# A selective-scan kernel of four layers: later pair sums, 64-row loads, all of them on one queue, new step positions and more buffers

## The chip, the cores and the metric

The kernel runs on one NeuronCore of a Trainium2 chip. The metric is the device time of one execution in microseconds (us). All times of instructions come from one profiled execution of the kernel; the kernel's own time is the median of three executions that were not profiled.

A core has five engines that take their instructions in order, each from its own queue: PE (matrix products; its weight loads are listed as PEld), DVE (vector), ACT (scalar functions), POOL (GpSimd) and SP, which computes nothing and issues DMAs. "SPq" and "ACTq" in a profile mean the queue of that engine: what it waits for or issues.

## The reference

The input has four images of 64 x 64 positions and 192 channels, in float32. Four residual layers follow each other, each on a group-normalised or layer-normalised input. Layers 0, 1 and 3 are selective state-space layers; layer 2 is a Toeplitz mixing layer that the change doesn't touch. What matters here is the scan that layers 0, 1 and 3 share, with 384 inner channels (192 in layer 3) and 16 states for each channel:

```python
def step(h, inp):
    d_t, b_t, c_t, u_t = inp
    dA = jnp.exp(d_t[:, :, None] * A)
    h = dA * h + (d_t * u_t)[:, :, None] * b_t[:, None, :]
    y = jnp.einsum('nds,ns->nd', h, c_t)
    return (h, y)
```

Here d_t is a softplus of a projection (called delta), and b_t and c_t are projections of the convolved input u. In layers 0 and 3 one scan runs over all 4096 positions of an image, in four directions (rows, columns, and both reversed). In layer 1 a sequence is one line of 64 positions, forward and reversed, of rows and then of columns; its output is y + u * D, times silu(z), times an output matrix, and the reversed directions are added to what the forward ones left in DRAM:

```python
u = silu(conv1d(u) + cb)
y = y + u * D
y = y * silu(z)
return einsum('nld,cd->nlc', y, out_w)
```

## The kernel before

**Units and jobs.** A job is a chunk of 512 positions in one direction. Layer 1 has 128 jobs (4 directions x 4 images x 8 chunks) that run as one list: 32 forward jobs on rows, 32 reverse jobs on rows, 32 forward and 32 reverse jobs on columns. Layers 0 and 3 have 32 jobs for each image. A job is cut into units (t, p, c): t is a block of 128 channels, c one half of it (64 channels), and p one of four groups of states; on the 128 partitions lie 64 channels x 2 halves of the states, and a unit's tile of 1024 columns holds two states for each. So a job of layers 0 and 1 has 24 units, one of layer 3 has 12.

**What one unit does.** `feed` builds the input b = delta * u * B in PSUM by matrix products with the diagonal matrices `diag` (L374, PE), and dA by two exponentials (L397, ACT). For the units named in `direct` (p = 3, in layer 1 and 3 for both c, in layer 0 for c = 1 only) b comes from POOL instead (`spread`, L347: dtu times B, both spread over the partitions by DMA), and dA is put into PSUM. `scan` runs the recurrence on DVE (L407 in layer 1, one instruction; L414 in layers 0 and 3, two, with a carry that ACT copies at L424 for the next job) and multiplies by C on POOL (L418). `collect` sums over states on PE with the matrix `fold` (L443), two units (a pair) in each of two steps n = 0, 1.

**Order of the work.** `run_jobs` writes the units down one after the other. At position i it feeds unit i + 2, scans unit i, spreads unit i + 3, and takes one entry from `waiting` to collect; a pair enters `waiting` when its second unit has been scanned, so its two sums stand at positions i + 1 and i + 2. Then the steps due at i are written; a step that returns a function gets that function run at i + 1. A job's other work stands at fixed positions before or after its first unit: `load` of its input, `input_of` (convolution, layer 1), `project` to B, C and delta, `turn_b`, `step_size` and `finish` (softplus, L269; then dtu = delta * u at L275, on POOL in layer 1, on DVE in layers 0 and 3), `turn` (transpose of dtu, L235 and L289), `gate` (z, L839), `gated` (u * D + y, L852, then times z, L853) and `out` (L877 to L888). In a layer 1 reverse job `earlier` (L869) loads what the forward direction left, and `out` adds to it. A scheduler then sets each engine's order from what was written and from its own times, so an instruction can stand a little earlier or later than written. Every DMA also waits for an earlier DMA that used the same one of eight completion semaphores.

**Loads.** `plan` gives each load a position: at least when its data is ready, at most 12 units ahead (`LEAD`), and, where its buffer has an earlier user, `behind` units after that user (3 in layers 0 and 3, 2 in layer 1). `fetch` issues them, all on SP: C (`c`, L335) and B (`bc`, L335), delta (`both`) and dtu (`dtu2`, called dtu in the profile where it is loaded). In layers 0 and 3 `both` and `dtu2` are copied from SBUF in pieces of at most 64 rows (L317). In layer 1 they come from DRAM, both halves of the partitions in one transfer of 128 rows of 2 KB:

```python
src = job["deltas" if name == "both" else "dtus"][key * 64 : (key + 1) * 64, :]
nc.sync.dma_start(one, src.unsqueeze(0).broadcast_to([2, 64, T]))
```

The stores that these loads read are issued by ACT for B, C (L226) and delta (L272), and by SP for dtu (L295). Layer 1 has buffers c=4, bc=2, diag=4, both=4, dtu2=2 and seven h tiles; layers 0 and 3 have three h tiles (and five hc tiles).

Of the kernel before, what the change touches and what calls it, by code (L numbers as in the profile page):

```python
# [7 lines left out]
F32 = mybir.dt.float32  # L8
# [8 lines left out]
N = 16  # L17
R = 12
E = R + 2 * N
T = 512  # L20
# [5 lines left out]
EARLY = 3  # L26
# [10 lines left out]
class Kernel:  # L37
# [66 lines left out]
    def run_jobs(self, jobs, pools):  # L104


        G = jobs[0]["DI"] // 64
        order = []
        for t in range(-(-G // 2)):
            order += [(t, *one) for one in (TWO if 2 * t + 1 < G else ONE)]  # L110
        units = [(k, *one) for k in range(len(jobs)) for one in order]
        per = len(order)
        steps = {}
        for k, job in enumerate(jobs):
            for at, step in self.prepare(job, pools) + job["steps"]:
                steps.setdefault(k * per + at, []).append(step)
        for at, load in self.plan(jobs, order, pools):
            steps.setdefault(at, []).append(load)
        start, end = min(steps), max(len(units) + 3, max(steps) + 1)
        waiting, rest = [], []  # L120
        for i in range(min(start, -EARLY), end + 4):
            if 0 <= i + AHEAD < len(units):
                k, t, p, c = units[i + AHEAD]
                self.feed(jobs[k], t, p, c, pools)
            todo = waiting[:1]
            if 0 <= i < len(units):
                k, t, p, c = units[i]
                after = self.scan(jobs[k], t, p, c, pools)
                if after is not None:
                    steps.setdefault(i + 1, []).insert(0, after)  # L130
            if 0 <= i + EARLY < len(units):
                k, t, p, c = units[i + EARLY]
                if c in jobs[k]["direct"].get(p, ()):
                    self.spread(jobs[k], t, p, c, pools)
            if 0 <= i < len(units):
                if (i + 1) % 2 == 0:
                    waiting += [(units[i][0], [one[1:] for one in units[i - 1 : i + 1]], n) for n in range(2)]


            if todo:  # L140
                k, two, n = waiting.pop(0)
                self.collect(jobs[k], two, n, pools)
                if n and two[1][1] == LAST:
                    steps.setdefault(i, []).append(lambda job=jobs[k], t=two[0][0]: job["add"](t))
            now, rest = rest + steps.pop(i, []), []
            for step in now:
                after = step()
                if after is not None:
                    rest.append(after)
        assert not rest and not steps and not waiting  # L150

    def plan(self, jobs, order, pools):


        uses, ready = {}, {}
        for k, job in enumerate(jobs):
            job["cbc"], job["bbc"], job["diag"], job["both"], job["dtu2"] = {}, {}, {}, {}, {}
            job["dtuT"] = {}
            when = {name: k * len(order) + at for name, at in job["when"].items() if isinstance(at, int)}

            near = 2 if job["carry"] is not None else 5
            dtu = when["finish"] + 3 if job["carry"] is not None else when["store"] + 5
            for j, (t, p, c) in enumerate(order):
                i, g = k * len(order) + j, 2 * t + c
                direct = c in job["direct"].get(p, ())
                reads = [("c", p, i, when["project"] + 6), ("both", g, i - AHEAD, when["finish"] + near)]
                if direct:
                    reads += [("bc", p, i - EARLY, when["project"] + 6), ("dtu2", g, i - EARLY, dtu)]
                else:
                    reads.append(("diag", p, i - AHEAD, when["turn_b"] + 5))  # L170
                for name, key, at, after in reads:
                    first, _ = uses.setdefault(name, {}).get((k, key), (at, at))
                    uses[name][k, key] = first, at
                    ready[name, k] = after
        loads = []
        for name, of in uses.items():
            bufs, turn = pools["bufs"][name], sorted(of, key=of.get)
            for j, (k, key) in enumerate(turn):
                first = of[k, key][0]
                at = max(ready[name, k], first - LEAD)  # L180
                if j >= bufs:
                    at = max(at, of[turn[j - bufs]][1] + pools["behind"])
                one = lambda part=None, job=jobs[k], name=name, key=key: self.fetch(job, name, key, pools, part)
                if name == "diag":


                    at = max(ready[name, k], first - (LEAD_DIAG if k else NB))
                    if j >= bufs:
                        at = max(at, of[turn[j - bufs]][1] + 3)
                    loads += [(first, at + part, lambda part=part, one=one: one(part)) for part in range(NB)]  # L190
                    at += NB - 1
                else:
                    loads.append((first, at, one))
                assert at < first, (name, k, key, at, first)
        return [one[1:] for one in sorted(loads, key=lambda one: one[0])]

    def prepare(self, job, pools):

        nc = self.nc
# [14 lines left out]
        def projected(ps):  # L214
# [8 lines left out]
            else:  # L223
                by_half = job["bc"].rearrange("a (h l) -> h a l", h=2)
            for h in range(2):
                nc.scalar.dma_start(by_half[h], xd[h * 64 : h * 64 + 2 * N, :])  # L226
            job["delta"] = prep.tile([P, NT, T], F32, name="delta", bufs=1)
            job["dtu"] = prep.tile([P, NT, T], F32, name="dtu", bufs=1)
            if P < 128:
# [37 lines left out]
        def finish():  # L267
            delta = job["delta"]
            nc.scalar.activation(delta, delta, AF.Softplus)  # L269
            if job["carry"] is None:  # L270
                job["deltas"] = self.bcd.tile([DI, T], F32, name="delta_dram")
                nc.scalar.dma_start(job["deltas"].rearrange("(t p) l -> p t l", p=P), delta)  # L272

            def after():
                (nc.gpsimd if job["carry"] is None else nc.vector).tensor_mul(job["dtu"], delta, job["u"])  # L275

            return after

        def turn(t):
            ps = mm.tile([128, NB, P], F32, name="dtu_ps", tag="mm")  # L280
# [16 lines left out]
        when = job["when"]  # L297
# [7 lines left out]
    def fetch(self, job, name, key, pools, part):  # L305
# [13 lines left out]
        elif name in ("both", "dtu2"):  # L319
            one = job[name][key] = pools[name].tile([128, T], F32, name=name)  # L320
            src = job["deltas" if name == "both" else "dtus"][key * 64 : (key + 1) * 64, :]
            nc.sync.dma_start(one, src.unsqueeze(0).broadcast_to([2, 64, T]))
        elif name == "diag":
            if part == 0:
                job["diag"][key] = pools["diag"].tile([128, NB, 4, 128], F32, name="diag")
# [74 lines left out]
    def scan(self, job, t, p, c, pools):  # L400
# [1 line left out]
        rev, carry, g = job["rev"], job["carry"], 2 * t + c  # L402
        way = slice(None, None, -1) if rev else slice(None)
        b, dA, direct = job["fed"].pop((t, p, c))
        h = pools["work"].tile([128, 2 * T], F32, name="h", bufs=7 if carry is None else 3)
        if carry is None:
            nc.vector.tensor_tensor_scan(h[:, way], dA[:, way], b[:, way], 0.0, ALU.mult, ALU.add)  # L407
        else:
# [143 lines left out]
    def ss2d_scan(self, pre, u_d, y_d, P, NT, ways, A, dtb):  # L552
# [3 lines left out]
        with (  # L556
# [10 lines left out]
            tc.tile_pool(name="s_y", bufs=2, space=PSUM) as yp,  # L567
        ):
            pools = {"prep": prep, "work": work, "c": cp, "diag": dp, "both": both, "mm": mm, "b": bp, "y": yp,
                     "bc": bcp, "dtu2": dtu2, "bufs": bufs, "behind": 3}  # L570
            jobs = []
            carry = {
                (g, p): pw.tile([128, 2], F32, name=f"carry{g}_{p}", bufs=1)
                for g in range(DI // 64) for p in range(PAIRS)
            }
            when = {
                3: dict(load=-33, project=-29, turn_b=-27, step_size=(-21, -19, -17), finish=-15,
                        turn=(-13, -11, -9), direct={3: (1,)}),
                2: dict(load=-25, project=-21, turn_b=-19, step_size=(-17, -16), finish=-14,
                        turn=(-9, -8), direct={3: (0, 1)}),  # L580
            }[NT]
# [122 lines left out]
    def mamba(self, x_in):  # L704
# [6 lines left out]
        done = [[self.dram.tile([C, L], F32, name=f"m_out{i}_{b}") for b in range(B)] for i in range(2)]  # L711

        both_w = [self.dram.tile([P, NT, C], F32, name=f"m_both_w{i}") for i in range(4)]
        bufs = dict(c=4, bc=2, diag=4, both=4, dtu2=2)
        with (
            tc.tile_pool(name="n", bufs=2) as pn,
            tc.tile_pool(name="n_ps", bufs=2, space=PSUM) as psum,
# [27 lines left out]
        with (  # L745
# [12 lines left out]
            tc.tile_pool(name="m_y", bufs=2, space=PSUM) as yp,  # L758
        ):
            pools = {"prep": prep, "work": work, "c": cp, "diag": dp, "both": both, "mm": mm, "b": bp, "y": yp,  # L760
                     "bc": bcp, "dtu2": dtu2, "bufs": bufs, "behind": 2}
            fixed = [once.tile([P, 2 * T], F32, name=f"dA{j}") for j in range(3)]
            zero = once.tile([P, 2 * ROWS], F32, name="zero")
            nc.gpsimd.memset(zero, 0.0)
# [13 lines left out]
    def mamba_job(self, pw, pin, mm, i, begin, rev, w, x, done, both_w, c, fixed, zero):  # L778
# [69 lines left out]
        def gated(t):  # L848

            def after():  # L850
                u, z = job["u"][:, t, :], job["z"][:, t, :]
                nc.vector.scalar_tensor_tensor(u, u, w["D"][:, t : t + 1], job["y"][t], ALU.mult, ALU.add)  # L852
                nc.gpsimd.tensor_mul(z, z, u)  # L853

            return after

        def parts(m):

# [30 lines left out]

            return after  # L890

        when = dict(project=-24, turn_b=-22, step_size=(-20, -19, -17), finish=-15, turn=(-9, -2, 3), store=-11)
        each = lambda f, ats: [(at, lambda t=t: f(t)) for t, at in enumerate(ats)]
        steps = [(-50, weights)] if begin else []
        steps += [(-46, load)] + each(input_of, (-37, -34, -31)) + each(gate, (-4, -1, 1)) + each(out, (30, 33))
        if rev:
            steps += each(earlier, (25, 28))
        job.update(
# [327 lines left out]
```

## Time and profile before

| What | Value |
|---|---|
| Median of three executions | 31300.29 us (31296.12 to 31304.8) |
| The profiled execution | 31284.29 us, of which the span from first to last instruction is 31282.5 us |
| Layer 0, first to last job start | 168 us to 10244 us |
| Layer 1, first to last job start | 10763 us to 21834 us |
| Layer 3, first to last job start | 25136 us to 31034 us |
| Busy over the span: PE, DVE, ACT, POOL | 87%, 71%, 74%, 73% |
| Mean granted TensorE clock | 0.952 |

A job's start is taken from the copy `xd` on ACT (L216), of which there is one for each job. A line of the groups names source line, engine, operation and operands (out<-in), its count, busy time and mean duration, and then the idle time of the engine just before and what ended it. A line of the waits reads: who waited, for whom, us in total, how many times, the longest. A line of a window gives the length of the stretch, and busy time with the number of instructions in brackets for PE, PEld, DVE, ACT and POOL, then the granted clock, the share of time in which the DMA engines moved data, and GB/s. A line of the timeline has start, duration, engine, line, operation, and the idle time before it. Durations on PE end at modelled times, and matrix products overlap.

### The profile page before, as it was taken

The numbers are of one execution on the slowest core, as the hardware profiler recorded it, in microseconds if no ns is written. First come the engines' busy times: TensorE is split into PE (matmuls) and PEld (weight loads), VectorE is DVE, ScalarE is ACT, GpSimd is POOL, SyncE is SP. The second block draws the span as 40 slices with busy tenths as digits, with TensorE's granted clock in tenths as the row PEclk, the third lists the DMA queues.
The fourth block names the chain that finished last, engine by engine and source line by source line (L and its number), as shares of the span: only waits on it lengthen the run. The fifth ranks groups of instructions, "written<-read, shape, count | busy, mean of one in ns | idle before, by whom it ended". The sixth has DMA issues, their size and how long they took to land. (4 is left out here: it accounts for less than half of the span.)

```text
span 31282.5 us, 503240 instructions
## 1 busy us (share of the span) xinstructions
PE 27353.4 (87%) x189464; PEld 16218.5 (52%) x189464; DVE 22344.0 (71%) x16587; ACT 23257.2 (74%) x50327; POOL 22884.2 (73%) x9831
## 2 busy tenths in 40 slices
PE   8998998998899699999889999998588988888888
PEld 5664654665466355555555555555355344444444
DVE  7887887888788677776667777676423277777777
ACT  7885885887688588887878888887232187878788
POOL 7885885888688499988889898888100077777777
PEclk9999999999999899999999999999799999999999
DMA  3333333333333433333333333333533344444444
GB/s 108 102 99 116 103 96 117 99 99 107 109 103 100 139 96 98 97 97 98 96 98 98 97 98 96 97 97 96 133 72 78 106 132 126 132 126 130 127 131 126
DMA packets 1606616, 3342.20 MB, mean 107 GB/s; under 512 B 350646, under 2 KB 407415, under 8 KB 1588567
## 3 DMA queue, kind: packets, MB, share of 16 engines
q1 hardware_dynamic: 1432150, 3033.08, 35.3%
q10 hardware_dynamic: 172032, 276.92, 2.6%
q8 instruction: 1497, 24.53, 0.3%
q14 instruction: 937, 7.67, 0.1%
HBM read 2149.81 MB, written 656.08 MB: 90 GB/s over the span
## 5 line engine op out<-in xcount | busy, mean ns | idle before, releaser
L374 PE MATMUL b<-diag,dtuT 128*64 128x256 f32 x98304 | 13308.4, 386 | 954.9 <-DVE h L414 759.4
L418 POOL TENSOR_TENSOR hc<-h,c 128x1024 f32<-128x1024 f32 x4608 | 10938.8, 2394 | 1641.9 <-DVE h L414 1336.6
L374 PEld LDWEIGHTS b<-diag,dtuT 128*64 128x64 f32 x98304 | 8544.2, 139 | 5362.7 <-issue 1770.1
L397 ACT ACTIVATE dA<-both,A 128x512 f32<-128x512 f32 (+1 forms) x12288 | 8308.5, 711 | 2062.3 <-DVE h L414 981.2
L414 DVE TENSOR_TENSOR_SCAN h<-dA,carry,b 128x512 f32<-128x512 f32 x6720 | 8180.2, 1263 | 1546.4 <-PE b L374 647.5
L418 POOL TENSOR_TENSOR h<-h,c 128x1024 f32<-128x1024 f32 x3072 | 7209.3, 2376 | 918.1 <-DVE h L407 570.0
L328 ACT ACTIVATE diag<-ident,bt 128x128 f32<-128x128 f32 x20480 | 6563.7, 391 | 106.9 <-issue 106.1
L407 DVE TENSOR_TENSOR_SCAN h<-dA,b 128x1024 f32<-128x1024 f32 x2304 | 5240.7, 2279 | 1701.4 <-PE b L374 829.2
L443 PE MATMUL y<-hc,fold 128*64 128x512 f32 x18432 | 5587.0, 605 | 534.0 <-POOL hc L418 533.3
L443 PE MATMUL y<-h,fold 128*64 128x512 f32 x12288 | 4736.9, 614 | 716.2 <-POOL h L418 713.0
L347 POOL TENSOR_TENSOR bs<-dtu,bc 128x1024 f32<-128x1024 f32 x1536 | 3642.2, 2371 | 452.8 <-issue 224.8
L497 POOL MEMSET pad<- 128x13068 f32 (+1 forms) x8 | 73.4, 9172 | 3974.3 <-DMA cw<-in_L_conv_w 3001.6
L443 PEld LDWEIGHTS y<-hc,fold 128*64 128x64 f32 x18432 | 1709.8, 139 | 1684.1 <-POOL hc L418 978.7
L397 ACT ACTIVATE b<-both,A 128x504 f32<-128x504 f32 (+1 forms) x3072 | 2074.0, 675 | 527.9 <-DVE h L414 438.3
L443 PEld LDWEIGHTS y<-h,fold 128*64 128x64 f32 x12288 | 1321.9, 139 | 1804.2 <-POOL h L418 1210.7
L407 DVE TENSOR_TENSOR_SCAN h<-b,bs 128x1024 f32<-128x1024 f32 x768 | 1752.7, 2282 | 650.8 <-ACT b L397 616.2
L414 DVE TENSOR_TENSOR_SCAN h<-b,carry,bs 128x512 f32<-128x512 f32 x1344 | 1638.8, 1260 | 111.8 <-ACT b L397 93.7
L235 PEld LDWEIGHTS dtu_ps<-ident,dtu 128*64 128x64 f32 (+1 forms) x16384 | 1165.4, 143 | 649.4 <-issue 307.6
L235 PE MATMUL dtu_ps<-ident,dtu 128*64 128x128 f32 (+1 forms) x16384 | 1309.6, 278 | 171.2 <-ACT z L839 125.3
L397 ACT ACT_TABLE_LOAD x1094 | 1403.6, 1283 | 15.2 <-DMA both<-delta_dram 2.6
L414 DVE TENSOR_TENSOR_SCAN h<-dA,b 128x512 f32<-128x512 f32 x960 | 1113.5, 1205 | 365.2 <-PE b L374 139.9
L275 DVE TENSOR_TENSOR dtu<-delta,u 128x1536 f32<-128x1536 f32 (+1 forms) x256 | 589.0, 2301 | 560.5 <-ACT delta L269 560.5
(157 smaller groups left out, 26136.2 us busy)
## 6 DMA issues: line engine op xcount, KB each, us to landing
c<-bc_dram SPq DMA_DIRECT2D x3072, 256.0 KB
both<-delta SPq DMA_DIRECT2D x2048, 128.0 KB
bc<-bc_dram SPq DMA_DIRECT2D x768, 256.0 KB
both<-delta_dram SPq DMA_DIRECT2D x768, 256.0 KB
dtu<-dtu_dram SPq DMA_DIRECT2D x768, 256.0 KB
dtu<-dtu SPq DMA_DIRECT2D x1280, 128.0 KB
L_y<-out ACTq DMA_DIRECT2D x512, 256.0 KB
u<-L_u SPq DMA_DIRECT2D x160, 768.0 KB
```

Source lines behind the costliest of these rows:

```text
L235: nc.tensor.matmul(to[half * 64 : (half + 1) * 64], of[:, half * 64 : (half + 1) * 64], self.ident[:p, :p], start=True, stop=True,)
L275: (nc.gpsimd if job["carry"] is None else nc.vector).tensor_mul(job["dtu"], delta, job["u"])
L328: nc.scalar.activation(to, self.ident, AF.Copy, scale=of)
L347: self.nc.gpsimd.tensor_mul(by(b), dtu, by(job["bbc"][p]))
L374: nc.tensor.matmul(to, dtu, job["diag"][p][:, k, 2 * q : 2 * q + 2, :], start=True, stop=True,)
L397: nc.scalar.activation(to[n], of, AF.Exp, scale=w["A"][:, g, 2 * p + n : 2 * p + n + 1])
L407: nc.vector.tensor_tensor_scan(h[:, way], dA[:, way], b[:, way], 0.0, ALU.mult, ALU.add)
L414: nc.vector.tensor_tensor_scan(hn[:, n, way], dA[:, n, way], by_n[:, n, way], start, ALU.mult, ALU.add)
L418: nc.gpsimd.tensor_mul(hc, h, job["cbc"][p])
L443: nc.tensor.matmul(y[c * 64 : (c + 1) * 64, :], self.fold, of, start=first == 0 and n == 0, stop=last == LAST and n == 1)
L497: nc.gpsimd.memset(pad, 0.0)
```

## The change

The pair sums of layer 1 are written one position later than before (`lag` 1: positions i + 2 and i + 3), those of layers 0 and 3 as before (`lag` 0). In layer 1 each `both` and `dtu2` load becomes two transfers of 64 rows, and the stores of B, C and delta are issued by SP; the store of delta is written one position later. `behind` is 3 there, with five c buffers and three dtu2 buffers. The steps of layer 1 stand elsewhere, and `gated` runs one position later. In layers 0 and 3 there are four h tiles, and dtu = delta * u stands one position later (with `near`, `dtu` and, in layer 0, `turn` moved along).

```diff
@@ run_jobs
-        for i in range(min(start, -EARLY), end + 4):
+        for i in range(min(start, -EARLY), end + 6):
...
-            todo = waiting[:1]
+            todo = waiting[:1] if waiting and waiting[0][0] <= i else []
...
-                    waiting += [(units[i][0], [one[1:] for one in units[i - 1 : i + 1]], n) for n in range(2)]
+                    two = [one[1:] for one in units[i - 1 : i + 1]]
+                    waiting += [(i + 1 + pools["lag"], units[i][0], two, n) for n in range(2)]
...
-                k, two, n = waiting.pop(0)
+                _, k, two, n = waiting.pop(0)
@@ plan
-            near = 2 if job["carry"] is not None else 5
-            dtu = when["finish"] + 3 if job["carry"] is not None else when["store"] + 5
+            near = 3 if job["carry"] is not None else 5
+            dtu = when["finish"] + 4 if job["carry"] is not None else when["store"] + 5
@@ prepare
-                nc.scalar.dma_start(by_half[h], xd[h * 64 : h * 64 + 2 * N, :])
+                dma = nc.sync if job["carry"] is None else nc.scalar
+                dma.dma_start(by_half[h], xd[h * 64 : h * 64 + 2 * N, :])
...
                 job["deltas"] = self.bcd.tile([DI, T], F32, name="delta_dram")
-                nc.scalar.dma_start(job["deltas"].rearrange("(t p) l -> p t l", p=P), delta)

             def after():
+                if job["carry"] is None:
+                    nc.sync.dma_start(job["deltas"].rearrange("(t p) l -> p t l", p=P), delta)
                 (nc.gpsimd if job["carry"] is None else nc.vector).tensor_mul(job["dtu"], delta, job["u"])

-            return after
+            return after if job["carry"] is None else lambda: after
@@ fetch
-            nc.sync.dma_start(one, src.unsqueeze(0).broadcast_to([2, 64, T]))
+            for q in range(2):
+                nc.sync.dma_start(one[q * 64 : (q + 1) * 64, :], src)
@@ scan
-        h = pools["work"].tile([128, 2 * T], F32, name="h", bufs=7 if carry is None else 3)
+        h = pools["work"].tile([128, 2 * T], F32, name="h", bufs=7 if carry is None else 4)
@@ ss2d_scan
-                     "bc": bcp, "dtu2": dtu2, "bufs": bufs, "behind": 3}
+                     "bc": bcp, "dtu2": dtu2, "bufs": bufs, "behind": 3, "lag": 0}
...
-                        turn=(-13, -11, -9), direct={3: (1,)}),
+                        turn=(-12, -10, -8), direct={3: (1,)}),
@@ mamba
-        bufs = dict(c=4, bc=2, diag=4, both=4, dtu2=2)
+        bufs = dict(c=5, bc=2, diag=4, both=4, dtu2=3)
...
-                     "bc": bcp, "dtu2": dtu2, "bufs": bufs, "behind": 2}
+                     "bc": bcp, "dtu2": dtu2, "bufs": bufs, "behind": 3, "lag": 1}
@@ mamba_job
                 nc.gpsimd.tensor_mul(z, z, u)

-            return after
+            return lambda: after
...
-        when = dict(project=-24, turn_b=-22, step_size=(-20, -19, -17), finish=-15, turn=(-9, -2, 3), store=-11)
+        when = dict(project=-24, turn_b=-22, step_size=(-21, -19, -18), finish=-14, turn=(-9, -3, 8), store=-11)
...
-        steps += [(-46, load)] + each(input_of, (-37, -34, -31)) + each(gate, (-4, -1, 1)) + each(out, (30, 33))
+        steps += [(-46, load)] + each(input_of, (-36, -34, -31)) + each(gate, (-6, -4, -1)) + each(out, (33, 35))
```

## The prediction

> **What bounds the kernel now.** I read busy time by stretch first: layer 0, layer 1 forward, layer 1 reverse, layer 3.
>
> ```profile
> 600.00:2200.00 1600.00, 1491.73 (x11768) 966.88 (x11766) 1374.55 (x1136) 1345.48 (x3346) 1417.67 (x607) 0.97 0.38 101
> 12000.00:13600.00 1600.00, 1474.84 (x10220) 866.71 (x10218) 1144.77 (x666) 1395.25 (x2532) 1434.17 (x636) 0.98 0.31 97
> 14500.00:16000.00 1500.00, 1348.15 (x9158) 758.37 (x9156) 1045.97 (x633) 1202.98 (x2222) 1284.71 (x569) 0.96 0.31 96
> 25500.00:26400.00 900.00, 785.42 (x5797) 471.33 (x5792) 710.74 (x597) 835.60 (x2137) 814.60 (x341) 1.00 0.49 132
> ```
>
> Nothing is full: in the forward stretch PE is busy 92%, POOL 90%, ACT 87%, DVE 72%; engines that take turns at waiting for each other. Next the xd copies, one a job, forward and then reverse:
>
> ```profile
> L216 ACT COPY xd<-xd_ps x19: 345/350/352, 12013.6 to 13558.1; 128x256 f32<-128x256 f32 x19
> ...
> L216 ACT COPY xd<-xd_ps x17: 348/372/373, 14532.8 to 15966.6; 128x256 f32<-128x256 f32 x17
> ```
>
> (13558.1 - 12013.6) / 18 = 85.8 us a forward job (most single periods are 85.3), 1433.8 / 16 = 89.6 us a reverse one. Both do the same POOL work, 0.896 x 85.8 = 0.856 x 89.6 = 77 us: that is the floor. Reverse jobs lose 4.3 us more to something. The waits of POOL, then of ACT, in the reverse stretch name it:
>
> ```profile
> POOL h L418 <- DMA c<-bc_dram: 76.3, 14, 7.4
> POOL bs L347 <- issue: 70.3, 15, 6.1
> POOL h L418 <- DVE h L407: 34.0, 26, 6.4
> ...
> POOL bs L347 <- DMA dtu<-dtu_dram: 10.2, 7, 5.4
> ```
> ```profile
> ACT dA L397 <- DMA bc_dram<-xd: 102.3, 16, 7.5
> ```
>
> Loads come late. SP's timeline shows them being issued late and slowly, up to 7.78 us for one issue where others take 0.5:
>
> ```profile
> 15000.55 2.76 SPq L322 DMA_DIRECT2D both<-delta_dram  x2
> 15003.41 7.78 SPq L322 DMA_DIRECT2D dtu<-dtu_dram  x1
> 15011.24 5.18 SPq L888 DMA_DIRECT2D m_out<-o  x1
> ```
>
> In the forward stretch DMA waits are small, and the waits of PE and of POOL close a circle: PE, in order, stands at a pair sum until POOL has multiplied, so the next b is late, so DVE is late, so POOL idles.
>
> ```profile
> PE y L443 <- POOL h L418: 93.7, 55, 3.5
> PE b L374 <- DVE h L407: 30.6, 40, 4.2
> ```
> ```profile
> POOL h L418 <- DVE h L407: 127.0, 91, 4.5
> POOL z L853 <- DVE u L852: 30.5, 19, 4.4
> ```
>
> Last, DVE's waits in layer 0, and one of layer 3:
>
> ```profile
> DVE h L414 <- PE b L374: 118.4, 134, 1.6
> DVE dtu L275 <- ACT delta L269: 30.4, 22, 1.4
> DVE h L414 <- ACT carry L424: 26.0, 26, 1.3
> DVE h L414 <- POOL hc L418: 20.6, 23, 1.1
> ```
> ```profile
> DVE h L414 <- ACT carry L424: 85.6, 86, 3.4
> ```
>
> **What the Trainium skill says.** "DMA: Bandwidth & Descriptors", section "Why a DMA increments its semaphore by 16 and not by 1": a transfer is split over the largest k up to 16 that divides the slowest dimension of both sides, and only those k engines report its landing. The layer 1 source has slowest dimension 2, so k = 2. The trace agrees: the landing records of all 1503 such loads that I could pair with their issue have 3 steps (one at once, two engines), those of the 64-row loads of layer 0 have 16. From issue to last landing the 128-row loads take 14.8 us (both) and 16.4 us (dtu) in the median, c loads beside them 12.5 us; in layer 0 a 64-row both takes 2.6 us and a c load 4.0 us. The same page, "Issuing engines are not separate DMA queues": another issuer saves only issue time. Here it also moves a wait (below). "ScalarE: Activation LUTs", "What ACT_TABLE_LOAD costs": 1283 ns and a drain of 1380 ns; the trace has 1283 ns loads and the next instruction right behind, so I use 1.283 us. "Perfetto Trace Analysis", "Identifying the Most-Contended Engine": matmul busy time misjudges PE; weight loads are 54% of the forward stretch, so I take POOL's 77 us, not PE's 79, as floor.
>
> **Part 1: 64-row loads, SP alone, more buffers, `behind` 3.** A job has 6 both and 6 dtu loads of 128 packets of 2 KB, that is 12 x 64 = 768 packets on each of two engines; such a packet takes 0.096 us in the mean: 74 us. Those engines' sixteenth of everything else is 0.20 x 89.6 = 18 us: 92 us in 89.6, so two engines are full (packets overlap a little) while all 16 average 31%. After: about 31% everywhere, and landings as in layer 0, some 3 to 4 us. With five c buffers and three dtu buffers the built order waits for users 5 to 6 units back and leaves 4 to 6 units, 14 us or more, before use. So reverse POOL loses its DMA waits: 76.3 + 10.2 + 1.4 (another bs row), and I count the 70.3 without a releaser, as bs waits for loads only: 158 / 16.7 jobs = 9.4 us. Not all is gained: DVE takes its place, as in the forward stretch (POOL's waits there are 157.5 / 18.65 = 8.5 us a job). Reverse falls to forward: -4.3 x 64 = -275 us. The moved stores free ACT, which had to stand at its B store (0.55 us issue) until loads of SP's had landed; the 102.3 us are in this sum. Price: 12 + 3 more issues on SP, 15 x 0.55 = 8 us a job, hidden in SP's idle time (its waits in the forward stretch are over 1,000 of 1,600 us). Behind the moved stores on SP stand both, dtu and C loads; each store waits for ACT's xd copy or softplus, which the order puts about 10 units before the first use.
>
> **Part 2: lag, steps, table loads (layer 1).** PE's 93.7 / 18.65 = 5.0 us a job at pair sums go to a sum that stands about a unit (3.5 us) later, longer than nearly every such wait; h tiles allow it (five of seven alive). The built order has 1674 table loads before in layer 1 and 1522 after: 152 x 1.283 = 195 us of ACT, 1.5 us a job, beside other work. PE's other products no longer stand in a row at 20 (z), 22 (turn), 23 (z), 0 (xd) and 1 (z). What is late next is POOL itself, with DVE behind ACT's exponentials for the direct units (137 us of its waits in the forward stretch, 7 us a job, untouched). Of the 8.5 us left above the floor I take a third, 2.8 us; bounds: +0.5 (a z product now waits for DVE's taps of the preceding `in`, a new wait) and -5.5. Both directions: -2.8 x 128 = -358 us. The last job's `out` stands 2 to 3 positions later with nothing beside it: +7 us once.
>
> **Part 3: layer 0.** A fourth h tile and the later dtu take 30.4 + 26.0 + 20.6 = 77 us of DVE's idle time in 22.4 jobs, 3.4 us a job of 71.5. PE and DVE wait for each other there (118 us for b), so most is passed on; I take 30%: -1.0 x 128 = -132 us; bounds 0 and -1.9.
>
> **Part 4: layer 3.** The carry wait is 85.6 / 22.8 = 3.75 us a job of 39.5, but ACT is busy 93% and idle only 2.8 us a job: -0.55 x 128 = -70 us; bounds 0 and -1.5.
>
> Sum: -275 - 358 + 7 - 132 - 70 = -828 us; 31284 - 828 = 30456 for the profiled execution. The median lies 16 us above that execution: 30472, rounded 30470.
>
> **Rivals.** (a) Only the DMA stall goes, parts 2 to 4 nothing: for it, the forward period is compute's and repeats to 0.1 us; against it, the 93.7 us. 31300 - 275 + 7 = 31030. (b) The circle breaks fully: part 2 at -5.5 x 128 = -704, part 3 at -243, part 4 at -192: 31300 - 275 - 704 - 243 - 192 + 7 = 29890. For: POOL's waits are nearly all for DVE; against: DVE's for ACT stay. (c) Slower: SP in one line becomes the late one. A store at its head waits for softplus, and the both loads behind miss their exponentials; ACT stands, as in the reverse jobs, up to 7.5 us. It decides only if SP falls 10 units (35 us) back. Then forward jobs pay 64 x 7.5 = 480 and reverse ones gain nothing: 31300 + 480 - 200 (parts 3, 4) = 31580. Against: SP's idle time. (d) The 64-row loads don't spread, or nothing else moves: 31300; layer 0's landings speak against it.
>
> **Chances.** Forecast 67% (30200 to 30800), (a) 12%, (b) 14%, (c) 4%, (d) 3%. The range 29950 to 31000 leaves out (c), (d), and about half of (a) and of (b), 2 in 10. Under 0.2% (63 us) is no change that a measurement of this kernel could tell: faster 0.93, same 0.03, slower 0.04.
>
> **What would show it.** Part 1: 16 landing steps for both and dtu in layer 1, SP issues near 0.55 us, no POOL waits for DMA above 10 us in a reverse stretch, and reverse jobs within 1 us of forward ones. Part 2: PE's wait at pair sums under 30 us in 1600, periods near 82.5 us, POOL busy 93%. Parts 3 and 4: no DVE wait for carry, hc or delta; periods near 70.5 and 39 us. I am wrong if reverse jobs stay above 88 us (the landings weren't it), or if the forward ones stay at 85 with PE's waits gone (then DVE behind ACT was the circle).

## The result, and the profile after

The changed kernel takes 30866.03 us (median, 30860.95 to 30871.51); the kernel before, run beside it, took 31302.54 us (31296.12 to 31310.67). The ratio is 0.986, with a 95% interval of 0.9843 to 0.9878: faster, by 436 us where 828 were predicted. Between the two profiled spans the gain is 31282.5 - 30864.0 = 418 us, and the starts of the jobs show where it lies: layer 1, first to last job start, 11070 to 10793 us (-278); layer 3, 5898 to 5767 us (-131); layer 0 +14; the gap from layer 1 to layer 3 -21; the tail -4.

First the same stretches as before: layer 0, layer 1 forward, layer 1 reverse, layer 3 (lengths, then busy time of PE, PEld, DVE, ACT, POOL, granted clock, DMA share, GB/s).

```profile
600.00:2200.00 1600.00, 1499.49 (x11712) 1048.17 (x11710) 1369.67 (x1130) 1338.85 (x3330) 1410.15 (x603) 0.97 0.39 101
12000.00:13600.00 1600.00, 1421.97 (x10244) 748.35 (x10244) 1159.50 (x673) 1338.10 (x2495) 1442.79 (x640) 1.00 0.34 98
14500.00:16000.00 1500.00, 1338.74 (x9635) 691.99 (x9631) 1102.23 (x672) 1247.46 (x2315) 1357.73 (x600) 1.00 0.36 102
25000.00:25900.00 900.00, 796.55 (x6010) 479.55 (x6008) 725.09 (x606) 868.51 (x2226) 839.79 (x350) 1.00 0.53 138
```

The reverse stretch has become like the forward one: POOL is busy 90.5% and 90.2%. In layer 3 ACT is now at 868.5 / 900 = 96.5%; in the same part of that layer before (25283:26183, as the layer began 283 us later) it was at 853.2 / 900 = 94.8%. The copies that mark a job's start, forward and reverse:

```profile
L217 ACT COPY xd<-xd_ps x19: 345/348/350, 12006.3 to 13540.1; 128x256 f32<-128x256 f32 x19
...
L217 ACT COPY xd<-xd_ps x17: 345/348/350, 14572.2 to 15937.5; 128x256 f32<-128x256 f32 x17
```

(13540.1 - 12006.3) / 18 = 85.2 us a forward job (85.0 in most) and 1365.3 / 16 = 85.3 us a reverse one, where 82.5 was forecast for both. The loads did what was expected. On the page's list of DMA issues they now have a landing time, the last column:

```profile
c<-bc_dram SPq DMA_DIRECT2D x3072, 256.0 KB, 4.1
...
both<-delta_dram SPq DMA_DIRECT2D x1536, 128.0 KB, 3.7
dtu<-dtu_dram SPq DMA_DIRECT2D x1536, 128.0 KB, 2.7
```

Before it was 12.5, 14.8 and 16.4 us in layer 1. (The median for c is over all layers; in layer 1 alone it is 4.1 us too.) The landing records of these `both` and `dtu` loads now fit 16 steps for each, where they had 3. SP's timeline in the reverse stretch has issues of about 0.6 us each (a row of x2 holds two) where one took up to 7.78 us:

```profile
15004.11 1.13 SPq L326 DMA_DIRECT2D dtu<-dtu_dram  x2
15005.34 0.54 SPq L339 DMA_DIRECT2D bc<-bc_dram  x1
15005.97 2.47 SPq L326 DMA_DIRECT2D both<-delta_dram  x4
```

In the reverse stretch neither POOL nor ACT waits for a DMA any more. PE's wait at the pair sums is gone too, as forecast. On the page the group of layer 1's sums (busy, mean ns, then idle time just before) had 716.2 us of idle time:

```profile
L447 PE MATMUL y<-h,fold 128*64 128x512 f32 x12288 | 3259.6, 593 | 10.2 <-POOL h L422 10.2
```

And yet the forward period stayed at 85. The waits of the forward stretch say who took PE's place (who waited, for whom, us, times, longest):

```profile
PEld b L378 <- DVE h L411: 279.3, 205, 8.4
ACT dA L401 <- DVE h L411: 215.4, 95, 11.6
DVE h L411 <- ACT b L401: 166.7, 60, 4.7
PE b L378 <- DVE h L411: 141.1, 131, 7.5
POOL h L422 <- DVE h L411: 135.5, 59, 4.1
DVE h L411 <- ACT dA L401: 109.6, 53, 4.6
```

DVE waits for ACT's exponentials 276 us, 14.7 us a job (231.5 us before), and ACT waits for DVE 215 us (57.9 before). The two wait for each other, in different parts of a job. ACT's timeline of one forward job, cut to the rows around its two long waits and to a stretch in which it never stops:

```profile
12383.97 1.32 ACT L401 ACTIVATE dA<-both,A 128x504 f32<-128x504 f32 x2 [3.67 <-DVE h L411]
...
12389.63 1.32 ACT L401 ACTIVATE dA<-both,A 128x504 f32<-128x504 f32 x2 [3.77 <-DVE h L411]
...
12411.01 1.28 ACT L401 ACT_TABLE_LOAD   x1
12412.31 1.32 ACT L401 ACTIVATE dA<-both,A 128x504 f32<-128x504 f32 x2
12413.65 1.28 ACT L843 ACT_TABLE_LOAD   x1
12414.94 0.60 ACT L843 ACTIVATE z<-z_ps 128x512 f32<-128x512 f32 x1
12415.44 2.44 ACT L332 ACTIVATE diag<-ident,bt 128x128 f32<-128x128 f32 x8
12417.88 1.28 ACT L401 ACT_TABLE_LOAD   x1
12419.18 1.32 ACT L401 ACTIVATE dA<-both,A 128x504 f32<-128x504 f32 x2
```

and DVE's scans behind it:

```profile
12420.53 2.29 DVE L411 TENSOR_TENSOR_SCAN h<-dA,b 128x1024 f32<-128x1024 f32 x1 [4.58 <-ACT dA L401]
12423.39 2.29 DVE L411 TENSOR_TENSOR_SCAN h<-dA,b 128x1024 f32<-128x1024 f32 x1 [0.57 <-ACT dA L401]
12429.50 2.29 DVE L411 TENSOR_TENSOR_SCAN h<-b,bs 128x1024 f32<-128x1024 f32 x1 [3.82 <-ACT b L401]
```

ACT stands still for 7.4 us at 12380 to 12390, released each time by a scan: it can run ahead of DVE only as far as there are dA tiles, three in layer 1. Later in the same job it has more to do than a unit's time allows: between the exponentials of one unit, which end at 12413.6, and those of the next, which begin at 12419.2, stand two table loads, a silu and eight parts of diagonal tiles. DVE stands for 4.6 and 3.8 us.

Three of DVE's waits in layer 0, and its two longest in layer 3:

```profile
DVE h L418 <- PE b L378: 161.8, 183, 2.2
...
DVE dtu L278 <- ACT delta L271: 29.8, 22, 1.4
...
DVE h L418 <- POOL hc L422: 11.7, 15, 1.0
```
```profile
DVE h L418 <- ACT dA L401: 54.3, 46, 3.9
...
DVE h L418 <- issue: 40.5, 30, 2.3
```

The carry waits are gone in both. In layer 0 the wait for b grew by 43 us in their place, and the later dtu is waited for as before; the job takes 71.7 us (71.6). In layer 3 a steady job of the second and fourth direction takes 37.2 us (40.1 before), one of the first and third 39.4 (39.3).

### The profile page after: what moved, and what is told of

It is laid out like the page before. It is cut to its first block, busy times and chain, and to the rows that moved or that the text cites. A ratio compares the mean times of both kernels' runs of the same rounds, so it can differ in the third digit from the quotient of the medians.

```text
span 30864.0 us, 503255 instructions
## 1 busy us (share of the span) xinstructions
PE 26878.4 (87%) x189464; PEld 15827.7 (51%) x189464; DVE 22327.6 (72%) x16587; ACT 23000.6 (75%) x50177; POOL 22890.6 (74%) x9831
## 5 line engine op out<-in xcount | busy, mean ns | idle before, releaser
L378 PE MATMUL b<-diag,dtuT 128*64 128x256 f32 x98304 | 12607.9, 386 | 1732.9 <-DVE h L411 917.9
L378 PEld LDWEIGHTS b<-diag,dtuT 128*64 128x64 f32 x98304 | 8214.9, 138 | 6212.3 <-DVE h L411 1903.3
L447 PE MATMUL y<-hc,fold 128*64 128x512 f32 x18432 | 5783.3, 599 | 386.1 <-POOL hc L422 384.4
L447 PE MATMUL y<-h,fold 128*64 128x512 f32 x12288 | 3259.6, 593 | 10.2 <-POOL h L422 10.2
L447 PEld LDWEIGHTS y<-hc,fold 128*64 128x64 f32 x18432 | 1924.0, 138 | 1550.1 <-POOL hc L422 813.1
L447 PEld LDWEIGHTS y<-h,fold 128*64 128x64 f32 x12288 | 1005.0, 137 | 795.2 <-issue 444.9
L827 DVE SCALAR_TENSOR_TENSOR u<-in_ps,conv_w,u 128x504 f32<-128x504 f32 (+2 forms) x1152 | 831.6, 722 | 411.7 <-ACT u L822 402.6
```

The costliest lines, as they stand in the source:

```text
L378: nc.tensor.matmul(to, dtu, job["diag"][p][:, k, 2 * q : 2 * q + 2, :], start=True, stop=True,)
L447: nc.tensor.matmul(y[c * 64 : (c + 1) * 64, :], self.fold, of, start=first == 0 and n == 0, stop=last == LAST and n == 1)
L827: nc.vector.scalar_tensor_tensor(u[:, :, to], ps[:, :, of], tap(3 - j), u[:, :, to], ALU.mult, ALU.add)
```

## Experiments

After the result I held that PE's place in the forward period had gone to ACT, with DVE behind it. Its rivals: that the loads had never been worth more than they gave, and that the lag or the new positions had themselves made the new wait. Each kernel ran beside the kernel before, whose median lay between 31293 and 31303 us in every series. Periods in us are those of steady jobs, in layer 1 a mean over 24 of them in each direction, in layer 3 those of the first and third direction, then of the second and fourth.

| kernel | median us | ratio to before, 95% interval | L1 forward | L1 reverse | L3 |
|---|---|---|---|---|---|
| before | 31302.5 | | 85.3 | 89.7 | 39.3 / 40.1 |
| changed | 30866.0 | 0.9843 to 0.9878 | 85.0 | 85.3 | 39.4 / 37.2 |
| before, 64-row loads | 30730.9 | 0.9803 to 0.9832 | 85.3 | 80.9 | 39.3 / 40.1 |
| the same, stores on SP | 30357.1 | 0.9683 to 0.9716 | 79.8 | 80.4 | 39.3 / 40.1 |
| before, 64-row loads, copy on DVE | 30444.3 | 0.9712 to 0.9745 | 80.9 | 80.8 | 39.3 / 40.1 |
| changed, 128-row loads | 31004.2 | 0.9892 to 0.9921 | 85.2 | 86.6 | 39.4 / 37.2 |
| changed, lag 0 | 30783.4 | 0.9819 to 0.9852 | 84.3 | 84.7 | 39.4 / 37.2 |
| changed, a quarter of diag's instructions | 30017.4 | 0.9576 to 0.9605 | 78.4 | 78.8 | 39.4 / 37.2 |
| changed, three h tiles | 31056.7 | 0.9909 to 0.9939 | 85.0 | 85.4 | 39.3 / 40.1 |
| changed, old positions | 30218.7 | 0.9641 to 0.967 | 79.7 | 80.3 | 39.4 / 37.2 |
| the same, lag 0, gated as before | 30233.7 | 0.9646 to 0.9675 | 79.8 | 80.4 | 39.4 / 37.2 |
| changed, old inputs, gates, outputs | 30460.0 | 0.9716 to 0.9748 | 81.9 | 82.0 | 39.4 / 37.2 |
| changed, old step sizes, softplus, turns | 30464.7 | 0.9719 to 0.9748 | 81.7 | 82.0 | 39.4 / 37.2 |
| old positions, copy on DVE | 30248.8 | 0.9652 to 0.9681 | 80.3 | 80.2 | 39.4 / 37.2 |

**The loads alone.** On the kernel before:

```diff
-            nc.sync.dma_start(one, src.unsqueeze(0).broadcast_to([2, 64, T]))
+            for q in range(2):
+                nc.sync.dma_start(one[q * 64 : (q + 1) * 64, :], src)
```

> The kernel before with one edit: each both and dtu2 load of layer 1 in two transfers of 64 rows. Theory (two full DMA engines were all that the change gained in layer 1): reverse jobs fall from 89.6 to about 85.3 us, forward jobs stay at 85.3, layers 0 and 3 stay: 31300 - 64 x 4.2 = 31030 us. Rival (the stores on ACT, which stands at their issue, or the short lead of behind 2 hold the reverse jobs up): less than half of it, 31170 us or more.

It gained 569 us, more than the whole change. The forward jobs didn't move; the reverse jobs fell to 80.9 us, far under the forward ones. So the late loads had hidden that the reverse jobs without them run at about 81 us, not at the forward stretch's 85.3. ACT and DVE run all of their instructions in the same order as in the kernel before, so a new order of theirs isn't the cause. POOL, in the reverse stretch of this kernel, waits almost only for DVE (and 4.7 us for a load of B); the longest waits there, cut:

```profile
DVE h L408 <- PE b L375: 138.6, 125, 5.0
ACT dA L398 <- DVE h L408: 118.0, 77, 4.0
...
POOL h L419 <- DVE h L408: 55.2, 45, 2.7
```

**The loads taken back.** The reverse edit, on the changed kernel.

> The changed kernel with one edit undone: the both and dtu2 loads of layer 1 are one transfer of 128 rows again. Theory (two full DMA engines): reverse jobs return to 89 us or more, forward ones stay near 85: 30866 + 64 x 4.2 = 31135 us. Rival (with stores on SP, more buffers and behind 3 the loads are early enough, whatever they take): 30870 to 30950 us.

Here the 128-row loads cost only 138 us, less than the theory's 270 and more than the rival's at most 84: they still cost the reverse jobs 1.3 us, but something else holds both directions at 85 already.

**The stores moved to SP.** The kernel with the loads alone, and

```diff
-                nc.scalar.dma_start(by_half[h], xd[h * 64 : h * 64 + 2 * N, :])
+                dma = nc.sync if job["carry"] is None else nc.scalar
+                dma.dma_start(by_half[h], xd[h * 64 : h * 64 + 2 * N, :])
...
-                nc.scalar.dma_start(job["deltas"].rearrange("(t p) l -> p t l", p=P), delta)
+                nc.sync.dma_start(job["deltas"].rearrange("(t p) l -> p t l", p=P), delta)
```

> The kernel before with the 64-row loads (30731 us, forward jobs 85.3, reverse ones 81.3) and one more part of the change: the stores of B, C and delta of layer 1 are issued by SP instead of ScalarE, at the same positions. The changed kernel with the old order (old places, no lag) has forward jobs of 80.1; besides the stores it has c and dtu buffers more, behind 3, and the delta store one position later. Theory A (ScalarE's issues, three of some 0.55 us a job and what it waits for there, held up the forward jobs): forward 80 to 81.5, reverse 79.5 to 81.3, total 30380 to 30500. Theory B (buffers and behind 3 did it, by when the loads are issued and where PE meets its waits): forward stays at 85.0 to 85.4, total 30680 to 30740.

Another 374 us, all from layer 1, and the forward jobs now run at 79.8. The waits of the forward stretch, first with the loads alone, then with the stores moved:

```profile
PE y L444 <- POOL h L419: 95.1, 56, 3.6
DVE h L408 <- ACT dA L398: 76.0, 23, 4.2
ACT dtuT L289 <- PE dtu_ps L235: 73.7, 20, 5.2
```
```profile
DVE h L409 <- ACT dA L399: 55.5, 29, 2.8
...
PE y L445 <- POOL h L420: 21.1, 41, 1.2
```

PE's waits at the sums, which the prediction wanted to remove by the lag, fell from 95.1 to 21.1 us without any lag, and ACT's wait for the transposed dtu went. The issues themselves took ACT little, 1.56 us a job:

```profile
12438.21 1.19 ACTq L226 DMA_DIRECT2D bc_dram<-xd  x2
12469.40 0.37 ACTq L272 DMA_DIRECT2D delta_dram<-delta  x1
```

That is less than the 5.5 us that the forward job gained. The scheduler ordered the engines anew without the stores (PE's products stand in another order within a job, and a forward job has 13 table loads on ACT, not 14, while a reverse one has 14, not 12.4), so how much is ACT's freed time and how much the new order stays open.

**Another relief of ACT.** The kernel with the loads alone, with the forward output's copy out of PSUM on DVE:

```diff
-                    nc.scalar.copy(o, ps)
+                    nc.vector.tensor_copy(o, ps)
```

> The kernel before with 64-row loads, and the copy of out in forward jobs on DVE in place of ACT, as reverse jobs have their sum there. Theory (forward jobs are 5 us longer than reverse ones with the same loads because ACT has 0.9 us more to do at out and sends its engines into another order): forward jobs fall to about 80 us: 30731 - 64 x 5 = 30410 us. Rival (the difference is of the direction itself, of the scans run backwards): forward jobs stay at 85, 30730 us.

The forward jobs fall to 80.9. The copy itself is 0.9 us a job; in the order that came with the edit ACT also has 12.4 table loads in a forward job, not 14, so that its busy time falls by 3.3 us, from 75.0 to 71.7. Two different reliefs of ACT each break the 85.3 us, which speaks for ACT as the weak place of the old forward order; that a small edit also lets the scheduler out of an unlucky order isn't excluded. The number of table loads alone isn't it: reverse jobs with 14 of them run at 80.4 in the kernel with the stores moved.

**No lag.** The changed kernel with `"lag": 0` for layer 1.

> The changed kernel with lag 0 in layer 1. Theory (ACT sets layer 1's pace in the changed kernel, so the pair sums' wait was not what the period hung on): PE's waits at the pair sums come back, some 5 us a job, and the period stays within 0.5 us of 85: 30870 us, give or take 60. Rival (the later sums keep the new order at 85): forward jobs at 87 us or more, 31100 us or more.

It is 83 us faster than the changed kernel, a little more than was expected. ACT's order within a forward job hardly changes with it, PE's does. With lag 0 DVE waits less for ACT (137.7 and 19.2 us in the forward stretch, 157 in all against 276), but 74.6 us for POOL, and PE waits at the sums again (38.2 us).

**The old positions.** The changed kernel with

```diff
-        when = dict(project=-24, turn_b=-22, step_size=(-21, -19, -18), finish=-14, turn=(-9, -3, 8), store=-11)
+        when = dict(project=-24, turn_b=-22, step_size=(-20, -19, -17), finish=-15, turn=(-9, -2, 3), store=-11)
...
-        steps += [(-46, load)] + each(input_of, (-36, -34, -31)) + each(gate, (-6, -4, -1)) + each(out, (33, 35))
+        steps += [(-46, load)] + each(input_of, (-37, -34, -31)) + each(gate, (-4, -1, 1)) + each(out, (30, 33))
```

> The changed kernel with the step positions of layer 1 as before (steps, gate, out, input); lag 1 and the later gated stay. Theory (the new step positions put reverse jobs from 80 to 85 us, by crowding table loads and diagonals on ACT): reverse jobs fall to 81 us or less: 30866 - 64 x 4 = 30610 us or less. Rival (the lag did it): reverse jobs stay at 84 or more, 30800 us or more.

It takes 647 us less than the changed kernel, 5 us in every job of layer 1. The waits of DVE and ACT in the forward stretch are half of what they were:

```profile
ACT dA L401 <- DVE h L411: 107.5, 53, 4.5
...
DVE h L411 <- ACT b L401: 71.0, 56, 4.3
...
DVE h L411 <- ACT dA L401: 54.2, 29, 2.8
```

DVE behind ACT is 125.2 us in 20 jobs, 6.3 us a job, against 14.7 with the new positions. POOL is nearly full:

```profile
12000.00:13600.00 1600.00, 1515.88 (x10960) 812.73 (x10960) 1236.17 (x726) 1462.40 (x2696) 1541.06 (x684) 0.99 0.37 105
```

It is busy 1541 of 1600 us: it has become the limit. ACT, over 24 steady forward jobs, has more to do here (73.1 us a job) than with the new positions (71.8), and yet the job is 5 us shorter: what the new positions cost comes from where ACT's work stands, not from how much it is. This kernel was the fastest complete one.

**The old order whole.** The same, with lag 0 and `gated` at its old place (`return after`).

> The changed kernel with the step positions, lag 0 and gated of before in layer 1; 64-row loads, stores on SP, behind 3, the buffers and all of layers 0 and 3 stay. Theory (positions, lag and gated are what took back the gain): forward 85.3, reverse about 80 us, layer 3 at 37.7 to 38.8: 30731 - 131 = 30600 us. Rival (the stores on SP, behind or the buffers cost it): reverse jobs at 84 or more, 30800 us or more.

30234 us, not the 30600 expected, as the forward jobs don't go back to 85.3. With the old positions lag and late `gated` together make 15 us, 0.05%, and the two intervals overlap: no difference is shown. Its layer 1 jobs equal those of the kernel before with loads and stores changed (79.8 and 80.4 in both, with ACT's instructions in the same order in their steady jobs), so more buffers and `behind` 3 are worth nothing that shows; the 123 us between those two kernels are those of layer 3.

**Which positions.** First inputs, gates and outputs back at their old places, then step sizes, softplus and turns instead (the two lines of the diff above, one at a time).

> The changed kernel with three of layer 1's steps back where they were before the change: the input projections with their taps at -37, -34, -31, the gates at -4, -1, 1 and the output projections at 30 and 33; step sizes, softplus and the transposes of delta*u stay at the new places. All of the new places back gave 30219 us (a job of 80.0 in both directions) against 30866 (85). Theory 1: the cost lies in the gates' move ahead of the step at -3, which packs taps, Silu, gates and the exps of the tables into one stretch of ScalarE; then this kernel takes most of the 650 back: 30250 to 30450, jobs of 80 to 82, and more than 1019 table loads. Theory 2: the cost lies in the third transpose at 8 instead of 3 and the softplus at -14: then 30750 to 30900, jobs of 84 to 85. A sum of both kinds gives 30500 to 30700.

> The counterpart: the changed kernel with step sizes at -20, -19, -17, softplus at -15 and the transposes of delta*u at -9, -2, 3 as before the change; inputs, gates and outputs stay at the new places. Theory 1 (the gates' move costs): 30750 to 30900, jobs of 84 to 85. Theory 2 (softplus and third transpose cost): 30250 to 30450, jobs of 80 to 82. If each half takes back only part, 30500 to 30700; if each alone takes back nearly all, the two moves bind only together, and the long stretch of ScalarE needs both.

30460 and 30465 us. Neither theory holds: each half of the new positions costs about 244 us when put on the good order (30460 - 30219 and 30465 - 30219), both together 647. Table loads don't decide it: the second kernel has as few of them (1019) as the changed one, the first 1113, and they take the same time.

**ACT lighter.** The changed kernel with one instruction in place of four for each part of a diagonal tile in layer 1, so that the diagonals of three of four states are left out:

```diff
+            if job["carry"] is None:
+                to, of = job["diag"][key][:, part], job["bt"][:, part, 4 * key : 4 * key + 1]
+                eye = self.ident.unsqueeze(1).broadcast_to([128, 4, 128])
+                nc.scalar.activation(to, eye, AF.Copy, scale=of)
+                return
```

> The changed kernel with work left out in layer 1: of the four diagonal matrices of a block only the first state's values are used, written by one ACT instruction of 512 columns in place of four of 128, so some 16 x 0.86 = 13.8 us less of ACT a job. Theory (ACT sets the pace in part of each job): the period falls toward POOL's 77 us, to about 80: 30866 - 128 x 5 = 30230 us. Rival (the order DVE, PSUM, ACT, DVE sets it by its latency, whatever else ACT does): 84 us or more, 30740 us or more.

The one instruction is longer (0.71 us against 0.39): ACT is busy with diagonal tiles 8.3 us a job instead of 15.7, so 7.4 us are saved, not the 13.8 that were expected. With the new positions and the lag untouched the job falls from 85.0 to 78.4 us, and POOL is busy 98% of the forward stretch:

```profile
12000.00:13600.00 1600.00, 1511.74 (x11136) 767.41 (x11134) 1264.57 (x734) 1319.29 (x1986) 1565.26 (x695) 1.00 0.37 107
```

So a relief of ACT frees the changed kernel's job, by about what was taken from ACT, and behind ACT stands POOL at about 77 us, the floor that the prediction named. It isn't a clean test of ACT's load: its other instructions stand in another order in this kernel, so how much is load and how much order stays open here too.

**Three h tiles in layers 0 and 3.** The changed kernel with `bufs=7 if carry is None else 3`.

> The changed kernel with three h tiles in layers 0 and 3 again. Theory (the fourth h tile alone is what layer 3 gained, as DVE there waited for the carry copy): layer 3 returns to 39.5 us a job, layer 0 stays at 71.7: 30866 + 130 = 31000 us. Rival (the later dtu step did it): within 40 us of 30866.

191 us slower. Layer 3's steady jobs are those of before again (39.3 and 40.1): all of its gain is the fourth h tile. In layer 0 the job takes 72.0: the later dtu with what moved beside it costs 0.4 us (71.6 before) and the fourth tile gives 0.3 back. DVE's waits there show the exchange; with three tiles

```profile
DVE h L418 <- PE b L378: 108.6, 120, 1.6
DVE dtu L278 <- ACT delta L271: 30.4, 22, 1.4
...
DVE h L418 <- ACT carry L428: 25.7, 36, 1.3
DVE h L418 <- POOL hc L422: 20.2, 21, 1.1
```

and with four, carry is gone and the wait for b is 161.8.

**Both reliefs.** The changed kernel with the old positions, and the forward copy on DVE.

> The changed kernel with all of layer 1's steps at their old places, and the forward direction's output copied from PSUM by VectorE instead of ScalarE. Theory A (what is left in layer 1 is GpSimd, 96% busy in both directions of the kernel with the old places alone): no gain, 30180 to 30260, jobs of 79.8 to 80.3. Theory B (ScalarE, at 91%, still holds up the forward direction as it did in the kernel before): the forward job falls by about 1 us, 64 jobs, 30120 to 30170.

30249 us, no gain: POOL limits there, and relief of ACT has nothing left to give.

## Why the prediction was right and wrong

**The direction** came from the loads, and their mechanism was read rightly: transfers over two of 16 engines, SP and POOL late because of it. All signs asked for in part 1 are there. Rival (c) did not happen: with all of the issues on SP, the waits of the four computing engines for DMAs come to 0.5 us in the forward stretch and none in the reverse one.

**"Reverse falls to forward"** (part 1, -4.3 a job) is the step that was mis-sized. Loads and stores alone give 85.3 to 79.8 forward and 89.7 to 80.4 reverse: 64 x (5.5 + 9.3) = 947 us, 941 measured (31298 - 30357), against 275. Two things were wrong in it. The forward period was taken for what compute needs, though it belonged to one order of work that a small relief of ACT broke; and the moved stores were counted "in this sum" of the reverse jobs, where they also freed the forward ones. POOL's 77 us floor and the 9.4 us of its DMA waits stood on the same page and pointed to 80 in the reverse jobs; I discounted them to 4.3.

**Part 2** (-2.8 a job for lag, positions and table loads) had the wrong sign. In layer 1 the old order, with the loads and stores changed, runs at 80; the new one at 85. Its 1.5 us a job fewer table loads brought nothing, and PE's wait did go, but DVE behind ACT took its place: the case the prediction named last, "forward ones stay at 85 with PE's waits gone". That wait was listed as "7 us a job, untouched". It was 12.3 us a job with the row for dA beside it, which was left out, and the new positions raised it to 14.7. The step that failed is that removing PE's waits lets the job fall towards POOL's floor: what came next was ACT, not POOL, and the bound of +0.5 for positions was about a tenth of their cost (647 / 128 = 5.1 us a job). That the positions cost this much is shown by taking them back. Why they do is seen in one job's timeline only, and the lighter ACT fits it; that the bunching of gates, diagonal tiles and exponentials is all of it was only argued, as with lag 0 waits for POOL and PE carry much of the loss.

So the -278 us of layer 1 lie near part 1's -275 by accident: 941 gained, 647 given back. That the total falls between 29950 and 31000 us is luck of the same kind. Rival (a), at 31030, came nearer to it than the forecast of 30470, but its reason, a forward period that is compute's own, fell as well.

**Part 3** (-132) gave nothing. DVE's dtu still waits 29.8 us for softplus: moved one position in what is written, it was not moved away from it on the engine. What the fourth tile frees goes to the wait for b. Its bound of 0 was right, the 30% was not.

**Part 4** (-70) gave -131. ACT's 2.8 idle us a job were taken as the bound; the tile brought 2.9 us a job in the second and fourth direction and nothing in the others, ACT going from 94.8% to 96.5% busy in the same part of the layer. (The prediction's 93% was read from another part.) The mechanism held; the term was half its size.

**The tail** (+7) was -4.

## What to carry to other kernels

A period that repeats to 0.1 us need not be compute's floor: compare it with the busy time of the fullest engine, and ask what an order of work costs before building on it. When two edits are made together, one can hide the other's gain: here loads and stores alone gave 941 us and the new positions took 647 back, and only single edits showed it. When a wait of one engine is removed, add up every wait of the next engine in line (all of DVE's rows for ACT, not the largest one), before letting the job fall to the floor.

## What the runs showed of the hardware

A transfer of 128 rows whose source had a slowest dimension of 2 took 14.8 to 16.4 us to land, with two DMA engines; two transfers of 64 rows, which move the same bytes, land in 2.7 to 3.7 us each. This agrees with the Trainium skill's "DMA: Bandwidth & Descriptors" ("Why a DMA increments its semaphore by 16 and not by 1"), by which the number of engines, at most 16, has to divide the slowest dimension of both sides: 3 landing steps became 16. The c loads beside them, which were not touched, went from 12.5 to 4.1 us in layer 1.

Moving 1.56 us of DMA issues or 0.9 us of copies off ACT shortened a forward job by 5.5 and 4.4 us, with the order of the engines and the number of table loads changed beside it; 15 DMA issues a job more on SP cost nothing that shows.
